# Layer-norm rows turned by DMA transposes of two 16-bit planes instead of TensorE, with the planner's buffers recut

## The chip, the cores and the metric

The kernel runs on one core of one Trainium2 chip. The metric is the device time of one execution in microseconds (us). Three runs of the kernel before took 3198.34, 3198.98 and 3199.27 us; their median, 3198.98 us, is the time before.

## The reference

64 graphs of 256 nodes with 256 features pass through four layers. Every layer begins with the same step, a layer norm over the features and a ReLU; its result goes through a graph network, and that is added to x.

```python
h = jnp.maximum(_layernorm(x, axis=-1), 0.0)
x = x + _L0_gnn_ref(h, adj, ...)     # 4 heads of attention, masked by adj, elu
h = jnp.maximum(_layernorm(x, axis=-1), 0.0)
x = x + _L1_gnn_ref(h, adj, ...)     # 4 heads of attention, a norm of each head
h = jnp.maximum(_layernorm(x, axis=-1), 0.0)
x = x + _L2_gnn_ref(h, adj, ...)     # 1 head of attention over 256 features
h = jnp.maximum(_layernorm(x, axis=-1), 0.0)
x = x + _L3_gnn_ref(h, adj, ...)     # 3 steps: h = GRU(adj^T @ (h @ W_i), h)
```

What matters here is that h is needed turned. It is computed with nodes on the 128 partitions (that is how the norm reduces over features), and the projections and the GRU's gates need the features on the partitions, since TensorE contracts over partitions.

## The kernel before, in words

The 64 graphs are cut into 33 units: the first and the last have one graph, the 31 between have two. `graphs(u, first, nb)` writes down all operations of a unit, with C = 2 nb chunks of 128 nodes. Nothing is issued there: each operation is recorded by `_Schedule.op` with its engine, an estimated cost in ns, the buffers that it reads and writes, and (for a DMA) its bytes. `_Schedule.run` then plays a list schedule over these estimates: on each engine the ready operation with the earliest due date goes next, a buffer of a class (`"xt"`, `"g"`, ...) is taken from a fixed number of slots when its first operation starts and given back when its last one is done, and the instructions are emitted in that order. The order on each of the five engines (TensorE, ScalarE, VectorE, GpSimd, and SyncE, here PE, ACT, DVE, POOL, SP) is therefore fixed in the program, and an instruction that waits holds up everything behind it on its engine. Changed costs or slot counts change the order, not the work.

A unit runs through these steps; several units are in flight, and xt slots bound how many:

- `layer0` loads x into `xt` and the adjacency into `at` by SP, makes the bfloat16 mask `am` and the cap `cap_n`, and turns the latter into `cap` by DMA transposes on SP (L1240, one for each chunk, 128 x 256 of 16 bits, 64 KB).
- `norm(xt, cls)`: DVE statistics (L997, L998), POOL's power (L1006, L1007), one small DVE operation, and ACT's scaled ReLU for each chunk (L1015) into one buffer `xn` (`hn` for the GRU).
- `transposed(xn, cls)`: for each half dc of the features, C turns of 128x128 fp32 on PE into one PSUM bank (L1032), and one ACT copy into `ht`, laid out as [P, DC, S]: half, then node (copies are recorded by the helper `vec`, so they show as L829).
- `project` (L1054): rows of `ht` times weights, two matmuls for each chunk, evicted by ACT into `wh`.
- `factors`: a row of scores is turned (L1111), exponentiated, written to DRAM by ACT's queue (`rd`) and read back by SP as a broadcast over all partitions (`cb`, L1124), for all heads at once. The first two units (`SPREAD`) make it on PE instead (L1092).
- `weights` (L1145, and the minimum with the cap in L829) and `attend_heads` (L1163) form the attention; layers 0, 1 and 2 do norm, turn, project, attend in this way, layers 0 and 1 with 4 heads.
- `gru`: the `hn` of the last norm is turned into the state `ht` and split into two rounded parts `hl` (ACT, then POOL) for `aggregate` (L1361); three GRU steps follow, with gates (L1375, 36 groups of two matmuls of 512 columns in a unit, each of which the trace shows as four passes), turns of the new state (L1389), and the store of `xt` by SP (L1449).

On SP's queue stand the loads of x and the adjacency, the cap transposes, the broadcasts `cb<-rd` and the stores.

## Time and profile before

| what | number |
|---|---|
| median of 3 runs | 3198.98 us |
| span of the profiled execution | 3198.1 us |
| PE MATMUL L1375, gates, 2376 + 2376 passes | 1063.0 + 1055.6 us busy |
| PE MATMUL L1032, turns of xn and hn, 128x128 | 768 + 256 instructions |
| PE idle, 0 to 200 us | 32.3 us |
| PE idle, 3000 to 3198 us | 15.4 us |
| granted PE clock, mean | 0.996 |
| DMA moved | 138.82 MB, mean 43 GB/s |
| cb<-rd loads on SP | 60 of 1024 KB, 30 of 256 KB, 3 smaller |

The page gives one profiled execution. "Busy" is the time in which an engine ran at least one instruction. A group's line has the count, the busy time, the mean of one instruction in ns, and the idle time of the engine ahead of the group with what ended it. For PE the mean is the time from the start of a matmul to its modelled end; matmuls overlap, so the spacing of their starts, which the chain of waits gives, is shorter. A line of the stretch view has the stretch, its length, the busy time and count of PE, PE's weight loads, DVE, ACT and POOL, then the granted PE clock, the DMA engines' share and GB/s.

### The profile page before, as it was taken

The page shows a single profiled execution, that of the slowest core. Times are in us where ns is not written, and L with a number is a line of the kernel's source. Part 1 is how long each engine was busy: PE and PEld are TensorE (multiplying, and loading weights), DVE is VectorE, ACT ScalarE, POOL GpSimd, SP SyncE. Part 2 cuts the span into 40 slices and gives each one's busy share as a digit, 9 for nine tenths or more (in the row PEclk, how much of TensorE's full clock was granted, in tenths as well). Part 3 has the DMA queues.
Part 4 walks back from the last instruction along what each step waited for, and adds up shares of the span by engine and source line. Part 5 has one row for each costly group of instructions (what it writes and reads, how often), then busy time and mean ns, then how long its engine had stood idle before and what let it go on. Part 6 is the DMA issues. An engine that isn't in the chain of part 4 may idle for free.

```text
span 3198.1 us, 48707 instructions
## 1 busy us (share of the span) xinstructions
PE 3143.2 (98%) x18599; PEld 1931.9 (60%) x18599; DVE 2321.4 (73%) x5206; ACT 1486.8 (46%) x3128; POOL 897.4 (28%) x907
## 2 busy tenths in 40 slices
PE   7899999999999999999999999999999999999998
PEld 6765656565666655566656566556566556665555
DVE  7777867778767778767678677788677787677753
ACT  5454444454454444454444454544444444544433
POOL 4323332133331233331233321333311333311210
PEclk9999999999999999999999999999999999999999
DMA  4110111101111101111101111111111011101000
GB/s 129 34 49 29 54 54 34 47 31 50 54 54 34 47 31 50 54 47 34 53 28 54 53 36 45 40 41 54 54 34 47 31 50 50 47 23 44 11 16 12
DMA packets 109927, 138.82 MB, mean 43 GB/s; under 512 B 44714, under 2 KB 97524, under 8 KB 102004
## 3 DMA queue, kind: packets, MB, share of 16 engines
q1 hardware_dynamic: 105712, 134.25, 12.8%
q8 instruction: 149, 2.44, 0.3%
q10 hardware_dynamic: 3972, 1.36, 0.2%
q14 instruction: 94, 0.77, 0.1%
HBM read 109.84 MB, written 17.34 MB: 40 GB/s over the span
## 4 chain that ended last, share of the span: by engine, by line
PE 87%; DVE 9%; POOL 2%; ACT 1%; issue 1%; DMA 0%; SPq 0%; ACTq 0%; POOLq 0%; DVEq 0%
PE bank L1375 55%; PE bank L1054 10%; PE bank L1163 10%; PE bank L1361 5%; PE bank L1032 3%; PE bank L1389 2%; DVE pt L1145 2%; DVE g L829 2%; DVE pt L829 1%; POOL mean L1297 1%; POOL o L829 1%; DVE o L829 1%; ACT ht L829 1%; DVE xt L1308 1%; DVE mean L829 1%
## 5 line engine op out<-in xcount | busy, mean ns | idle before, releaser
L1375 PE MATMUL bank<-ag,wc 128*128 128x512 f32 (+1 forms) x2376 | 1063.0, 582 | 0.0
L1375 PE MATMUL bank<-ht,whh 128*128 128x512 f32 (+1 forms) x2376 | 1055.6, 580 | 2.2 <-ACT g L829 1.3
L829 ACT ACTIVATE g<-bank,bg 128x512 f32<-128x512 f32 (+1 forms) x594 | 395.2, 670 | 713.6 <-PE bank L1375 706.6
L1375 PEld LDWEIGHTS bank<-ag,wc 128*128 128x128 f32 x2376 | 441.4, 190 | 459.2 <-issue 441.1
L1375 PEld LDWEIGHTS bank<-ht,whh 128*128 128x128 f32 x2376 | 435.0, 190 | 438.9 <-issue 424.2
L1006 POOL TENSOR_SCALAR mv<-mv 128x4 f32<-128x4 f32 (+1 forms) x132 | 81.9, 621 | 1428.6 <-DVE mv L998 1383.6
L1145 DVE TENSOR_SCALAR pt<-cb,f 128x256 f32<-128x256 f32 x1152 | 416.9, 430 | 6.0 <-ACT cb L1099 5.2
L1163 PEld LDWEIGHTS bank<-wh,pt 128*64 128x64 f32 (+1 forms) x8704 | 345.6, 142 | 94.4 <-issue 76.1
L829 DVE SCALAR_TENSOR_TENSOR g<-g,g 128x512 f32<-128x512 f32 (+1 forms) x396 | 263.3, 670 | 180.4 <-ACT g L829 180.4
L1163 PE MATMUL bank<-wh,pt 128*64 128x65 f32 (+1 forms) x8704 | 382.0, 233 | 9.7 <-DVE pt L829 5.8
L829 DVE TENSOR_TENSOR pt<-pt,cap 128x1024 f32<-128x1024 f32 (+1 forms) x297 | 341.3, 1193 | 0.1
L829 DVE SCALAR_TENSOR_TENSOR g<-bank,g 128x512 f32<-128x512 f32 (+1 forms) x198 | 129.8, 666 | 280.2 <-PE bank L1375 280.0
L829 DVE SCALAR_TENSOR_TENSOR g<-g,ht 128x512 f32<-128x512 f32 (+1 forms) x198 | 136.5, 689 | 172.0 <-ACT g L829 171.6
L1361 PE MATMUL bank<-am_r,hl 128*128 128x256 f32 x1536 | 238.1, 304 | 0.1
L1015 ACT ACTIVATE xn<-xt,mv 128x256 f32<-128x256 f32 x384 | 197.3, 588 | 72.1 <-DVE mv L829 71.9
L1361 PEld LDWEIGHTS bank<-am_r,hl 128*128 128x128 f32 x1536 | 198.2, 189 | 42.5 <-issue 30.6
L829 ACT COPY ag<-bank 128x512 f32<-128x512 f32 (+1 forms) x198 | 113.4, 573 | 233.4 <-PE bank L1361 230.1
L829 ACT ACTIVATE g<-g,bg 128x512 f32<-128x512 f32 (+1 forms) x198 | 137.6, 709 | 161.6 <-DVE g L829 159.4
L997 DVE BATCH_NORM_STATS2 st<-xt 128x6 f32<-128x256 f32 x512 | 208.1, 406 | 6.4 <-DMA xt<-in_x_dram 6.2
L829 ACT COPY ht<-bank 128x512 f32<-128x512 f32 (+1 forms) x264 | 137.8, 573 | 124.0 <-PE bank L1032 123.8
L1136 POOL MEMSET wh<- 128x16 f32 (+3 forms) x99 | 11.8, 120 | 635.5 <-ACT f L1130 635.5
L1007 POOL TENSOR_TENSOR mv<-mv,nhalf 128x4 f32<-128x4 f32 (+1 forms) x132 | 176.0, 1333 | 11.0
(91 smaller groups left out, 3452.2 us busy)
## 6 DMA issues: line engine op xcount, KB each, us to landing
cb<-rd SPq DMA_DIRECT2D x60, 1024.0 KB
xt<-in_x_dram SPq DMA_DIRECT2D x31, 512.0 KB
at<-in_adj_dram SPq DMA_DIRECT2D x31, 512.0 KB
out_dram<-xt SPq DMA_DIRECT2D x31, 512.0 KB
cb<-rd SPq DMA_DIRECT2D x30, 256.0 KB
cap<-cap_n SPq DMA_TRANSPOSE x128
cb<-rd SPq DMA_DIRECT2D x2, 512.0 KB
rd<-row ACTq DMA_DIRECT2D x60, 8.0 KB
```

What stands on the lines that cost most here:

```text
L829: emit = lambda: fn(*[a() if callable(a) else a for a in args], **kw)
L997: nc.vector.bn_stats(st.tile[:, c, :], xt.tile[:, c, :])
L1006: nc.gpsimd.tensor_scalar(mv.tile[:, 2, :], mv.tile[:, 1, :], 1e-5, None, op0=OP.add)
L1007: nc.gpsimd.tensor_tensor(mv.tile[:, 2, :], mv.tile[:, 2, :], nhalf[:, :C], op=OP.pow)
L1015: op("act", 610, lambda: nc.scalar.activation(xn.tile[:, c, :], xt.tile[:, c, :], AF.Relu, bias=mv.tile[:, 3, c : c + 1], scale=mv.tile[:, ...
L1032: nc.tensor.transpose(ps.tile[:, c * P : (c + 1) * P], xn.tile[:, c, dc * P : (dc + 1) * P], ident)
L1054: nc.tensor.matmul(ps.tile[:, : heads * W], lhsT=ht.tile[:, dc, c * P : (c + 1) * P], rhs=we[:, dc].rearrange("p h w -> p (h w)"), start=( ...
L1145: nc.vector.tensor_scalar(pt.tile[:, b, jc, :].rearrange("p (i n) -> p i n", n=P), cb.tile[:, h, 2 * b : 2 * b + 2, :], f.tile[:, 1, h, c ...
L1163: nc.tensor.matmul(ps[q * Q : (q + 1) * Q], lhsT=pt.tile[:, b, jc, i0 : i0 + Q], rhs=wh.tile[:, h, 2 * b + jc, :w], start=(jc == 0), stop= ...
L1361: nc.tensor.matmul(ps.tile[:, b * N : (b + 1) * N], lhsT=hl.tile[:, k, 2 * b + sc, :], rhs=am.tile[:, 2 * b + sc, :], start=(k == 0 and sc ...
L1375: nc.tensor.matmul(ps.tile[:, :S], lhsT=w[:, dc, g * P : (g + 1) * P], rhs=v.tile[:, dc, :], start=(first and dc == 0), stop=(last and dc ...
L1389: nc.tensor.transpose(ps.tile[:, c * P : (c + 1) * P], ht.tile[:, j, c * P : (c + 1) * P], ident)
```

## The change

From unit 4 on (`TURNED`), the four norms' rows are turned by SP instead of PE. A fp32 word is two 16-bit words. For each graph (two chunks, 128 x 512 words) ACT copies the low halves and the high halves into two planes `pl` (a 16-bit copy at a stride of two), one DMA transpose on SP turns all eight 128x128 blocks of the two planes into `tp` (256 KB), and a second ACT copy joins the planes into `ht`. The bits stay as they were. Units 0 to 3 still turn on PE, with the four turns of a graph in one bank instead of the C turns of a feature half.

Buffers are cut by graph: `norm` gives a list of [P, 2, D] buffers, `ht` is [P, C, DC, P] (chunk, half, node), `project` waits for its own graph's half, the GRU's first `hl` are cut by graph, and the broadcast `cb` is loaded in pieces of two heads. `hn` and the unused `ident_h` go; the slots of xt, am, cap, xn go up; those of cb (in bytes), hl and g go down. Some POOL cost estimates are changed.

```diff
+TURNED = 4
...
-            "xt": (slots, 5), "at": (slots, 1), "am": (slots, 4), "cap": (slots, 3),
-            "cap_n": (slots, 1), "xn": (slots, 2), "ht": (slots, 2), "wh": (slots, 3),
-            "cb4_": (slots, 2), "cb1_": (slots, 1), "pt": (slots, 4), "o": (slots, 2),
-            "ag": (slots, 2), "ht3_": (slots, 3), "hn": (slots, 1),
-            "hl": (slots, 3), "am_r": (slots, 1), "g": (slots, 9), "f": (slots, 6),
+            "xt": (slots, 6), "at": (slots, 1), "am": (slots, 6), "cap": (slots, 4),
+            "cap_n": (slots, 1), "xn": (slots, 4), "ht": (slots, 2), "wh": (slots, 3),
+            "cb2_": (slots, 2), "cb1_": (slots, 1), "pt": (slots, 4), "o": (slots, 2),
+            "ag": (slots, 2), "ht3_": (slots, 3), 
+            "hl": (slots, 2), "am_r": (slots, 1), "g": (slots, 8), "f": (slots, 6),
...
-            "mean": (slots, 4), "rd": (dram, 4), "bank": (banks, 8),
+            "mean": (slots, 4), "pl": (slots, 2), "tp": (slots, 2), "rd": (dram, 4), "bank": (banks, 8),
...
-            xn = buf(cls, [P, C, D])
+            xns = [buf(cls, [P, 2, D]) for _ in range(nb)]
...
-            op("pool", 1350, power, parts(mv, range(C)), [(mv, "r")])
+            op("pool", 700 + 320 * C, power, parts(mv, range(C)), [(mv, "r")])
...
-            ht = buf(cls, [P, DC, S])
+            ht = buf(cls, [P, C, DC, P])
...
+            def turned(b):
+                pl, tp = buf("pl", [P, 2, 2 * D], U16), buf("tp", [P, 2, 2 * D], U16)
+
+                def planes(flat):
+                    return flat.bitcast(U16).rearrange("p (n k) -> p k n", k=2)
+
+                op("act", 1150, lambda: nc.scalar.copy(
+                    pl.tile, planes(xns[b].tile.rearrange("p c d -> p (c d)"))), [xns[b]], [pl])
+                dma("sp", 1 << 18, lambda: nc.sync.dma_start(
+                    tp.tile.rearrange("p k (m n) -> p (k m) n", n=P), pl.tile.rearrange("p k n -> p (k n)"),
+                    transpose=True,
+                ), [pl], [tp], cost=4700)
+                op("act", 1150, lambda: nc.scalar.copy(
+                    planes(ht.tile[:, 2 * b : 2 * b + 2].rearrange("p c d n -> p (c d n)")), tp.tile,
+                ), [tp], [(ht, b)])
+
+            for b in range(nb):
+                (flipped if u < TURNED else turned)(b)
             return ht
...
-                op("pe", 895, emit, [ht, B_we], [ps], takes=[wh])
+                op("pe", 895, emit, [(ht, c // 2), B_we], [ps], takes=[wh])
...
-            cb = buf(f"cb{heads}_", [P, heads, C, P])
+            K = min(heads, 2)
+            cbs = [buf(f"cb{K}_", [P, K, C, P]) for _ in range(heads // K)]
...
-                op("pool", 1350 + 200 * C, power, [], [var])
+                op("pool", 630 + 520 * C, power, [], [var])
...
-                hl = buf("hl", [P, 2, C, P], F32R)
+                hl = buf("hl", [P, 2, C, P] if engine == "dve" else [P, 2, 2, D], F32R)
...
                         nc.tensor.matmul(
-                            ps.tile[:, :S], lhsT=w[:, dc, g * P : (g + 1) * P], rhs=v.tile[:, dc, :],
+                            by_chunk(ps.tile[:, :S]), lhsT=w[:, dc, g * P : (g + 1) * P], rhs=block(v, dc),
...
-            ht = transposed(hn, "ht3_")
+            hls = [split(lambda hn=hn: hn.tile, "pool", [hn]) for hn in hns]
+            ht = transposed(hns, "ht3_")
             ag = buf("ag", [P, DC, S])
             for dc in range(DC):
-                aggregate(ag, split(lambda dc=dc: hn.tile[:, :, dc * P : (dc + 1) * P], "pool", [hn]), dc)
+                aggregate(ag, hls, dc, lambda k, b, sc, dc=dc: hls[b].tile[:, k, sc, dc * P : (dc + 1) * P])
```

## The prediction

> **What bounds the kernel now.** I read the page's busy shares and its chain of waits first, then the costliest groups by shape, then a stretch of the chain in order of time, last the stretches around one set of DMA transposes.
>
> ```profile
> PE 3143.2 (98%) x18599; PEld 1931.9 (60%) x18599; DVE 2321.4 (73%) x5206; ACT 1486.8 (46%) x3128; POOL 897.4 (28%) x907
> ...
> PE 87%; DVE 9%; POOL 2%; ACT 1%; issue 1%; DMA 0%; SPq 0%; ACTq 0%; POOLq 0%; DVEq 0%
> PE bank L1375 55%; PE bank L1054 10%; PE bank L1163 10%; PE bank L1361 5%; PE bank L1032 3%; PE bank L1389 2%; DVE pt L1145 2%; DVE g L829 2%; DVE pt L829 1%; POOL mean L1297 1%; POOL o L829 1%; DVE o L829 1%; ACT ht L829 1%; DVE xt L1308 1
> ```
>
> TensorE is busy 98% and carries 87% of the chain; the turns that the change touches (L1032) are 3% of it. In every 200 us stretch from 200 to 2800 us PE is busy for 199.4 us or more. So a microsecond taken from PE shortens the run, and one put on another engine costs only if PE then waits for it. The pattern repeats every 96.9 us, one unit of two graphs (sets of cap transposes start at 1400.73, 1497.63 and 1594.53).
>
> ```profile
> L1032 PE MATMUL bank<-ident,xn 128*128 128x128 f32 x768 | 104.6, 277 | 16.5 <-ACT xn L1015 16.5
> ...
> L1032 PE MATMUL bank<-ident,hn 128*128 128x128 f32 x256 | 33.9, 273 | 0.3 <-ACT hn L1015 0.2
> L829 ACT COPY ht<-bank 128x512 f32<-128x512 f32 x248 | 132.5, 585 | 119.6 <-PE bank L1032 119.5
> ...
> L1214 ACT ACTIVATE cap_n<-at 128x1024 bf16<-128x1024 int32 x31 | 32.8, 1058 | 16.7 <-DMA cap<-cap_n 16.7
> ```
> ```profile
> 1525.00 0.88 PE bank L1032 x8
> ...
> 1569.47 0.87 PE bank L1032 x8
> ```
>
> The mean of 273 ns is the latency of one turn; they overlap. What counts is spacing: eight take 0.87 us on the chain, 0.109 each.
>
> ```profile
> L1240 SPq DMA_TRANSPOSE cap<-cap_n x128: 1167/1232/2462, 16.0 to 2855.6; - x128
> ```
> ```profile
> 1404.00:1405.00 1.00, 1.00 (x7) 0.86 (x6) 0.97 (x6) 0.00 (x0) 0.00 (x0) 1.00 0.31 66
> 1405.00:1406.00 1.00, 1.00 (x9) 0.94 (x8) 0.97 (x5) 0.00 (x0) 0.00 (x0) 1.00 0.21 40
> 1406.00:1407.00 1.00, 1.00 (x7) 0.73 (x6) 1.00 (x5) 0.45 (x1) 0.00 (x0) 1.00 0.19 42
> 1407.00:1408.00 1.00, 1.00 (x3) 0.38 (x2) 1.00 (x4) 0.14 (x1) 0.00 (x0) 1.00 0.00 0
> ```
> ```profile
> SPq L1124 <- DMA rd<-row: 1977.2, 93, 47.5
> ...
> SPq L1449 <- DVE xt L829: 300.8, 32, 58.0
> ```
>
> A transpose of 64 KB (two blocks of 128x128) holds SP's queue for 1.232 us. The four from 1400.73 are issued by 1405.77; at 1407 the DMA engines (last two columns: share, GB/s) are still, so a landing trails its issue by at most 1.23 us. SP mostly waits, in order, for others.
>
> **Removed from PE.** Units 4 to 31 have two graphs and 4 norms x 8 turns; unit 32 has half: 28 x 32 + 16 = 912 turns x 0.109 = 99.4 us. Bounds: by busy time (138.5 / 1024 = 0.135) 123 us; by the low edge of the chain's 3% (2.5% x 3198.1 x 912/1024) 71. I take spacing, since other matmuls close up to it.
>
> **ACT.** 224 copies of 0.585 and 8 small ones of some 0.38 go: -134 us. Added: 228 blocks (28 x 8 + 4), each with a split and a join of 1024 elements per partition. The nearest row is the 1.058 us of the 128x1024 group: 456 x 1.058 = +482. ACT comes to 1835 us, 59% of 3100. No row shows 16-bit words at a stride; were they twice as slow ACT would come to 2317, 75%, still not the bound. What hides it is PE's own work; uncovered, it costs what is in the chain below.
>
> **SP and DMA.** A block is 256 KB, eight 128x128 pieces, four times the row: 4 x 1.232 = 4.93 us of queue, 228 x 4.93 = 1124 us. Per unit: 8 x 4.93 + 5.04 (cap) + some 7 issues of 0.38 = 47 us of a period that should become 96.9 - 3.5 = 93.4. The engines' share rises by about 0.31 x 39.4 / 93.4 = 0.13 from 0.13 to 0.14. Neither fills. In the built order of a steady period SP has two turns, the at load, three turns, the out store, three turns, three cb loads, xt, four cap transposes, two cb loads. Three turns thus stand behind the store, which waits for another unit's last update of xt, and cb loads stand behind up to three turns (15 us). The cb loads in halves add two issues, 0.8 us, on a half-empty queue.
>
> The Trainium skill speaks against the change: "VectorE: DVE Perf Modes", section "The three transpose paths", puts a 128x128 16-bit transpose at 1309 ns by DMA and 390 by TensorE, and its rules keep DMA for where PSUM is not acceptable as the destination. The trace disagrees with the first (1232 ns for two pieces) and, in a dense stream of fp32, with the second (109 ns spacing). By the page a block would be 10.5 us and a unit 84 + 8 = 92 us of SP, so SP would be as full as PE and the time would stay near 3199 or above; by the row it is 3100. The measured row decides.
>
> **The wait that could be late.** From a unit's last attention rows to the first gate on its hn: reciprocal 0.16, xt 0.47, stats 0.6, power 0.64 + 1.37, mv 0.16, four applies 2.4, split 1.06, two blocks in SP's queue 9.86, landing 1.23, join 1.06 = 19 us. In the built order PE has between those two points: 13 gate groups of 1.72 (four passes of 0.43), w0 projection 3.56, two heads 2.02, two aggregates 1.88, turns 1.0 = 31 us. So 12 us to spare; three turns of another unit ahead (15 us) would use it up. At the end of the run the last unit, one graph, needs about 13 us and has 9 x 1.72 = 15.5. I take 0 in the steady part (bounds -0.8 to +1 us a unit, -22 to +28: below, the period is 96.9 while the spacings of its PE rows sum to about 96.1, and a part of that gap is waits for the copies that go; above, one wait of 1 us a unit) and +2 at the end (0 to 6, a whole late block).
>
> **Strides.** The first GRU layer reads ht in four runs of 128 columns. A column takes 0.85 ns in a 128-wide turn (0.109) and 0.84 in a 512-wide gate (0.43), so run length costs nothing in these rows: 0. DVE reads o and wh in pieces at 703 ns against 707 for the gate product: 0.
>
> **Buffers.** xt and am for six, half-size cb and hl, g at eight: no instruction, only order. A unit's way lengthens by some 7 us (first block) to 12 (second) for each of four norms, 47 at most; six slots instead of five give 6 x 93.4 - 5 x 96.9 = +76 us, so this covers itself. Fewer g and hl could stall DVE; the bound of 1 us a unit above holds that too. At the start other work comes first in the order: 0, bounds of 5 us either way, against 32 us of PE idle in the first 200.
>
> **Sum.** 3198.1 - 99.4 + 2 = 3100.7, in the profiled execution's own span; the median of the runs stands 0.9 above it: 3101.6, said as 3101.
>
> **The rivals.**
> *Turns land late: slower.* The change saves 8 x 0.109 = 0.87 us of PE per norm of two graphs, and there are 114 such norms' worth (912 / 8). From 0.87 us of waiting per norm on it is a loss. The place is SP's queue: turns behind the out store or behind each other. At 2 us a norm the time is 3199 + 114 x 1.13 = 3328. For it: SP runs in order, and the store waited 300.8 us for xt, once 58. Against: 12 us of slack, and SP half empty.
> *Another engine takes part of the chain.* DVE, POOL and ACT hold 12% of it, mostly in stretches where PE is busy 99% all the same: two chains of nearly one length. If half of the saving is taken by them, 3199 - 50 = 3150.
> *More than the turns goes.* With 0.135 per turn, or with the waits for the ht copies gone too (22 us): 3199 - 122 = 3077.
> *It does not do what it says.* The order shows no turns on PE after unit 3's, so this is only the case that PE's clock falls; granted is 1.00 in all steady stretches. Not weighed.
>
> **How the numbers follow.** Forecast 3101, 60%, with its own range 3078 to 3130 (the -22 and the +28); more goes 12%; another engine 14%; late 14%. Most of the late case is above 3199, and 2 of its points lie within 0.2% (6.4 us, about what a measurement here can tell from no change); another engine gives 1 there. So faster 0.85, same 0.03, slower 0.12. The range runs from 3070 to 3160: it takes in the bounds, 3077 and 3150, and leaves out most of the late case.
>
> **What would show it.** Turns: L1032 down to some 112 instructions and PE's busy time lower by 99 to 123 us, PE again at 199 us or more in steady stretches of 200, the period of cap transposes at 93.4. ACT near 1835; each new transpose near 4.93 us on SP, landing about 1.2 later. If PE's groups wait for ACT ht or its join, the late case holds; if a block takes over 10.5 us on SP (8 of them and the rest then fill 93), SP is the bound. I am wrong if steady stretches of PE show more than 1 us idle per unit.

## The result and the profile after

The changed kernel takes 3239.48 us (median of four runs, 3238.88 to 3240.06), against 3199.12 us for the kernel before in the same series: a ratio of 1.0126, 95% interval 1.0111 to 1.014. It is slower by 40 us; the forecast was 98 us faster.

The first view is the page's busy shares and chain of waits.

```profile
span 3237.6 us, 47649 instructions
...
PE 3104.5 (96%) x17687; PEld 1851.3 (57%) x17687; DVE 2416.1 (75%) x5205; ACT 1830.6 (57%) x3346; POOL 875.9 (27%) x905
...
PE 67%; DVE 27%; ACT 2%; issue 2%; POOL 1%; DMA 0%; ACTq 0%; SPq 0%; DVEq 0%; POOLq 0%
```

PE has its 912 turns less, but its busy time fell by only 38.7 us and the span around it grew. DVE, which the change hardly touches, is busy 95 us longer and holds 27% of the chain instead of 9%. The next views are steady stretches of PE (length, busy time and count, granted clock, DMA share, GB/s), one of the kernel before and two of the changed kernel.

```profile
1000.00:1200.00 200.00, 199.65 (x1166) 1.00 0.13 44
```
```profile
1000.00:1200.00 200.00, 194.27 (x1085) 0.98 0.27 65
1600.00:1800.00 200.00, 194.27 (x1092) 1.00 0.26 64
```

PE idles 5.7 us in 200 where it idled 0.35, and the granted clock is no longer 1.00 throughout. What PE waits for (engine, line, releaser: total us, times, longest):

```profile
PE bank L1408 <- ACT ht L1055: 46.0, 25, 2.6
PE bank L1408 <- ACT g L829: 25.4, 45, 1.6
PE bank L1422 <- DVE ht L829: 21.0, 8, 4.5
PE bank L1034 <- ACT xn L1015: 19.2, 4, 9.7
```

The last row is of the first units, which still turn on PE, and is not new (16.5 us before). The largest wait is for the new join (L1055), 25 times, about once a unit: that looks like turns that land late. But the queue's rows (minimum, median and maximum ns) and ACT's rows for split and join say otherwise:

```profile
L1051 SPq DMA_TRANSPOSE tp<-pl x228: 1231/1237/3098, 125.5 to 3156.3; - x114
```
```profile
L1055 ACT COPY ht<-tp 128x1024 uint16<-128x1024 uint16 x228 | 304.4, 1336 | 0.0
L1049 ACT COPY pl<-xn 128x1024 uint16<-128x1024 uint16 x228 | 234.2, 1040 | 0.0
```

A block of 256 KB holds SP's queue for 1.24 us, a quarter of what was reckoned, and ACT is never idle ahead of a join (0.0): the turns are there, the join stands late in ACT's order. The timeline shows what is late (start, length, engine, line, operation; "x7" are seven in a row; in brackets the idle time ahead and what ended it). This stretch comes back every unit.

```profile
1636.07 2.50 POOL L829 TENSOR_TENSOR o<-o,gamma_b 128x512 f32<-128x512 f32 x2
1636.13 1.23 DVE L829 SCALAR_TENSOR_TENSOR mv<-mv 128x4 f32<-128x4 f32 x1 [0.58 <-POOL mv L1007]
...
1639.04 5.25 DVE L1172 TENSOR_SCALAR pt<-cb,f 128x256 f32<-128x256 f32 x7
...
1640.32 2.54 POOL L829 TENSOR_TENSOR o<-o,beta_b 128x512 f32<-128x512 f32 x2
...
1642.81 2.61 POOL L829 TENSOR_TENSOR hl<-xn,hl 128x512 fp32r<-128x512 f32 x2
...
1644.21 1.76 DVE L829 SCALAR_TENSOR_TENSOR g<-g,g 128x512 f32<-128x512 f32 x1
...
1645.90 2.98 DVE L1172 TENSOR_SCALAR pt<-cb,f 128x256 f32<-128x256 f32 x9
1646.07 0.69 ACT L829 ACTIVATE g<-bank,bg 128x512 f32<-128x512 f32 x1 [2.38 <-DVE g L829]
...
1650.65 0.72 ACT L829 ACTIVATE g<-g,bg 128x512 f32<-128x512 f32 x1 [2.66 <-DVE g L829]
...
1652.71 1.33 ACT L1055 COPY ht<-tp 128x1024 uint16<-128x1024 uint16 x1
...
1654.09 1.12 PE L1408 MATMUL bank<-ht,whh 128*128 128x512 f32 x2 [1.86 <-ACT ht L1055]
```

While POOL runs its power, beta and hl, seven weights of DVE take 5.25 us; the nine after POOL has stopped take 2.98 us. The mean of the seven hides two kinds, as the row of the weights alone shows (minimum, median and maximum ns, first and last start), in the changed kernel and in the run e16 below, where POOL waits:

```profile
L1172 DVE TENSOR_SCALAR pt<-cb,f x7: 401/403/1405, 1639.0 to 1642.9; 128x256 f32<-128x256 f32 x7
```
```profile
L1182 DVE TENSOR_SCALAR pt<-cb,f x7: 398/402/403, 1684.0 to 1686.0; 128x256 f32<-128x256 f32 x7
```

The first four start before beta and take 0.40 us each, beside the power too. The three beside beta and hl take 1.35 to 1.41 us, each about as long as one operation of POOL (1.26 to 1.32 us). The same holds over the whole trace of the changed kernel: the 175 weights that overlap one of POOL's long operations (bias, gamma, beta, hl) take 1043 ns in the mean, the other 977 take 409. In the kernel before, 30 of the 1152 meet one.

A gate product takes 1.76 instead of 0.68 us. So DVE is about 4 us late, ACT waits 2.38 and 2.66 us for DVE's gates, the join behind them in ACT's order is late, and PE waits 1.86 us. The price is more than the wait. One period earlier, in stretches of 1 us (after the length the busy time and count of PE, PE's weight loads, DVE, ACT, POOL, then the granted clock, DMA share and GB/s):

```profile
1553.00:1554.00 1.00, 0.44 (x2) 0.00 (x0) 1.00 (x3) 1.00 (x3) 0.00 (x0) 1.00 0.00 0
1554.00:1555.00 1.00, 0.00 (x0) 0.00 (x0) 1.00 (x2) 1.00 (x2) 0.00 (x0) 1.00 0.03 8
1555.00:1556.00 1.00, 0.70 (x2) 0.46 (x3) 0.68 (x2) 1.00 (x3) 0.00 (x0) 1.00 0.07 16
1556.00:1557.00 1.00, 1.00 (x4) 0.52 (x3) 0.96 (x4) 1.00 (x3) 0.00 (x0) 0.84 0.54 109
1557.00:1558.00 1.00, 1.00 (x2) 0.37 (x2) 0.93 (x5) 1.00 (x3) 0.00 (x0) 0.50 0.82 153
...
1559.00:1560.00 1.00, 1.00 (x2) 0.34 (x1) 1.00 (x3) 1.00 (x2) 0.92 (x2) 0.50 0.00 0
1560.00:1561.00 1.00, 1.00 (x4) 0.41 (x3) 1.00 (x3) 0.59 (x1) 0.72 (x1) 0.95 0.00 0
```

After 1.86 us without PE (0.56 + 1.00 + 0.30) the clock falls to 0.50 and comes back in the slice from 1560: about 3.4 us at half speed, some 1.7 us of PE's work lost on top of the wait. Not every such wait does this: after the one at 1654.09, just as long, the clock stays at 1.00. In slices of 4 us, 15 units between 400 and 2800 us show a fall.

That reading left three theories. **A**: the work of POOL and DVE on the port that the plan calls `port` meets, and DVE pays. **B**: the plan's 4.7 us for a block puts joins too late in ACT's order. **C**: the fewer slots of g and hl stall the gates.

### The profile page after: what moved, and what is told of

Same layout as the page of the kernel before. It is cut to its first block, busy times and chain, and to the rows that moved or that the text cites. A ratio compares the mean times of both kernels' runs of the same rounds, so it can differ in the third digit from the quotient of the medians.

```text
span 3237.6 us, 47649 instructions
## 1 busy us (share of the span) xinstructions
PE 3104.5 (96%) x17687; PEld 1851.3 (57%) x17687; DVE 2416.1 (75%) x5205; ACT 1830.6 (57%) x3346; POOL 875.9 (27%) x905
## 4 chain that ended last, share of the span: by engine, by line
PE 67%; DVE 27%; ACT 2%; issue 2%; POOL 1%; DMA 0%; ACTq 0%; SPq 0%; DVEq 0%; POOLq 0%
PE bank L1408 44%; PE bank L1190 8%; PE bank L1073 8%; DVE pt L1172 6%; DVE g L829 5%; PE bank L1387 4%; DVE st L997 3%; DVE xt L829 2%; PE bank L1422 2%; DVE o L829 2%; DVE mv L998 1%; DVE pt L829 1%; DVE mean L829 1%; DVE ht L829 1%; DVE mv L829 1%
## 5 line engine op out<-in xcount | busy, mean ns | idle before, releaser
L1408 PE MATMUL bank<-ht,whh 128*128 128x512 f32 (+1 forms) x2376 | 1087.0, 597 | 49.4 <-ACT ht L1055 46.0
L1408 PE MATMUL bank<-ag,wc 128*128 128x512 f32 (+1 forms) x2376 | 1048.5, 583 | 23.3 <-ACT g L829 23.3
L1408 PEld LDWEIGHTS bank<-ht,whh 128*128 128x128 f32 x2376 | 448.5, 195 | 531.2 <-issue 435.8
L1172 DVE TENSOR_SCALAR pt<-cb,f 128x256 f32<-128x256 f32 x1152 | 501.8, 506 | 80.2 <-PE bank L1190 73.6
L829 DVE SCALAR_TENSOR_TENSOR g<-g,g 128x512 f32<-128x512 f32 (+1 forms) x396 | 303.9, 769 | 175.8 <-ACT g L829 175.8
L1015 ACT ACTIVATE xn<-xt,mv 128x256 f32<-128x256 f32 x512 | 274.2, 594 | 96.3 <-DVE mv L829 92.4
L1055 ACT COPY ht<-tp 128x1024 uint16<-128x1024 uint16 x228 | 304.4, 1336 | 0.0
L1049 ACT COPY pl<-xn 128x1024 uint16<-128x1024 uint16 x228 | 234.2, 1040 | 0.0
L1006 POOL TENSOR_SCALAR mv<-mv 128x4 f32<-128x4 f32 (+1 forms) x132 | 51.5, 390 | 672.5 <-DVE mv L998 607.4
L829 POOL TENSOR_TENSOR o<-o,bias_b 128x512 f32<-128x512 f32 (+1 forms) x66 | 85.8, 1301 | 538.6 <-DVE o L829 538.6
L997 DVE BATCH_NORM_STATS2 st<-xt 128x6 f32<-128x256 f32 x512 | 207.0, 404 | 6.0 <-DMA xt<-in_x_dram 5.7
```

What stands on the lines that cost most here:

```text
L829: emit = lambda: fn(*[a() if callable(a) else a for a in args], **kw)
L997: nc.vector.bn_stats(st.tile[:, c, :], xt.tile[:, c, :])
L1006: nc.gpsimd.tensor_scalar(mv.tile[:, 2, :], mv.tile[:, 1, :], 1e-5, None, op0=OP.add)
L1015: op("act", 610, lambda: nc.scalar.activation(xns[c // 2].tile[:, c % 2, :], xt.tile[:, c, :], AF.Relu, bias=mv.tile[:, 3, c : c + 1], sca ...
L1049: op("act", 1150, lambda: nc.scalar.copy(pl.tile, planes(xns[b].tile.rearrange("p c d -> p (c d)"))), [xns[b]], [pl])
L1055: op("act", 1150, lambda: nc.scalar.copy(planes(ht.tile[:, 2 * b : 2 * b + 2].rearrange("p c d n -> p (c d n)")), tp.tile,), [tp], [(ht, b)])
```

## The experiments

All are edits of the changed kernel unless said otherwise. A "port operation" is one that the code marks `port=True`. The plan starts none while another is running on DVE or POOL (`if (not o.port or self.port_free <= clock) and self.roomy(o)` in `_Schedule.run`), but nothing in the program enforces that on the chip: each engine runs its own order as soon as its operands are there.

| run | us | ratio to before, 95% interval | DVE busy, us |
|---|---|---|---|
| changed kernel | 3239.48 | 1.0111 to 1.014 | 2416.1 |
| e1 turns on PE | 3189.66 | 0.996 to 0.9985 | 2274.9 |
| e2 SP cost 1240 | 3253.55 | 1.0144 to 1.0203 | 2362.8 |
| e5 slots back | 3235.34 | 1.0087 to 1.0146 | 2416.1 |
| e6 POOL narrow | 3123.30 | 0.9738 to 0.9794 | 2274.9 |
| e7 POOL narrow and scratch | 3232.84 | 1.0092 to 1.0126 | 2398.9 |
| e3 POOL costs back | 3205.85 | 1.0014 to 1.0033 | 2359.6 |
| e8 power planned as port | 3237.13 | 1.0107 to 1.0141 | 2378.4 |
| e9 port held in order | 3138.93 | 0.9799 to 0.9832 | 2270.1 |
| e10 and power held | 3358.15 | 1.0483 to 1.0518 | 2274.4 |
| e11 before, port held | 3195.82 | 0.9983 to 1.0002 | 2240.7 |
| e12 true costs, port held | 3172.32 | 0.9903 to 0.9936 | 2255.8 |
| e13 e8 with port held | 3181.18 | 0.9932 to 0.9965 | 2263.0 |
| e14 and addition held | 3145.35 | 0.9815 to 0.9848 | 2262.7 |
| e15 only addition held | 3227.45 | 1.0072 to 1.0106 | 2400.8 |
| e16 only POOL waits | 3125.69 | 0.9754 to 0.9787 | 2302.8 |
| e17 turns on PE, port held | 3185.66 | 0.9945 to 0.9973 | 2243.9 |
| e18 true costs, POOL waits | 3167.80 | 0.9889 to 0.9925 | 2269.7 |
| e19 turns on PE, POOL waits | 3185.83 | 0.9946 to 0.9976 | 2244.2 |

### Four first looks: the turns, the estimate, the slots, POOL's load

**e1: every row turned on PE, the rest of the change kept.**

```diff
-TURNED = 4
+TURNED = 99
```

> The changed kernel with all turns left on TensorE (the unit from which SP turns is set past the last one): buffers by graph, slots, the 8-bit mask and the planner's other estimates stay as changed. Theory A (DVE and POOL meet on their shared port because the new order lets them overlap, whoever turns): DVE's pt group stays near 0.50 us a piece and the time is 3230 or more. Theory B (the turn's joins come late on ACT, since the planner reckons 4.7 us of SP for a transpose that takes 1.24): with no joins the time is 3199 within 10, DVE near 2320 us busy. Theory C (fewer g and hl slots, smaller cb): well over 3199, 3220 or more, with waits for buffers on DVE or ACT.

3189.66 us, PE busy 200.00 of 200 us in steady stretches, DVE back at 2274.9 us. The recut buffers, estimates and order are worth about 8 us by themselves; the loss comes only with the turns off PE. This is what B expected, and it refutes A in the form "whoever turns": with the turns on PE 33 weights meet POOL's long operations, with the turns off it 175.

**e2: SP's estimate set to what the trace shows.**

```diff
-                ), [pl], [tp], cost=4700)
+                ), [pl], [tp], cost=1240)
```

> The changed kernel, the planner told 1240 ns for a block's transpose in place of 4700; nothing else. Theory B: joins move up in ACT's order, PE's waits for the join (46 us by PE, 68 by its weight loads) fall under 20 us and the time falls to 3150 or less. Theory A: DVE's pt group stays near 0.50, joins wait less but the time stays within 3200 to 3250. Theory C: no change, about 3237.

3253.55 us, slower still. The waits for joins are gone, others come in (DVE waits 115.1 us for streamed `cb`), and DVE is still busy 2362.8 us. B, which expected 3150 us or less, is refuted as the whole cause. A fits only in part: the time lies 4 us above its range, and the weights take 440 ns in the mean, not 500.

**e5: the slots of hl and g as before.**

```diff
-            "hl": (slots, 2), "am_r": (slots, 1), "g": (slots, 8), "f": (slots, 6),
+            "hl": (slots, 3), "am_r": (slots, 1), "g": (slots, 9), "f": (slots, 6),
```

> The changed kernel with hl at 3 and g at 9 slots again, as before the change. Theory C: 3180 or less. Theories A and B: within 30 us of 3239, in either direction, as the order changes by chance.

3235.34 us, the same within the intervals, where C expected 3180 or less. C is refuted.

**e6: POOL's bias, gamma and beta of the first layer cut to 16 elements of a partition.** Order and estimates are unchanged. Most of these three operations is left out.

```diff
-                vec(nc.gpsimd.tensor_tensor, pool(1290), lambda: o.tile[:, hs], lambda: o.tile[:, hs],
-                    lambda: each(gamma_b), op=OP.mult, reads=[B_gamma], writes=part, engine="pool", port=True)
+                vec(nc.gpsimd.tensor_tensor, pool(1290), lambda: o.tile[:, hs, :1, :8], lambda: o.tile[:, hs, :1, :8],
+                    lambda: each(gamma_b)[:, :, :1, :8], op=OP.mult, reads=[B_gamma], writes=part, engine="pool", port=True)
```

> The changed kernel in the very same order on all engines, but POOL's bias, gamma and beta of layer 1 touch 16 elements in place of 512 (the rest of the product with gamma and of the sums is left out; these inputs have gamma one, bias and beta zero). It takes some 245 us of POOL's port use away. Theory A: DVE's pt group goes back to some 0.43 us, DVE's busy time falls by 60 us or more, PE's idle in the steady stretches falls from 5.7 to under 3 us per 200, and the time falls by 50 us or more. Theory B: the joins still stand behind ACT's other work and the time falls by less than 25. Theory C: by less than 25.

3123.30 us, 116 us under the changed kernel; DVE 141 us less busy; the weights take 431 ns in the mean and PE idles under 0.7 of 200 us, as A expected. This fits A, but also another reading: gamma and beta stand on a chain that ends at hl, and the cut made POOL's results earlier.

**e7: the load put back, the earliness kept.** Full-width additions on a scratch tile that nobody reads, one after the bias and two after the beta, follow the cut operations. Left out is the same as in e6.

```diff
+    def scratch(n, w):
+        for _ in range(n):
+            nc.gpsimd.tensor_tensor(scr[:, :w], scr[:, :w], scr[:, :w], op=OP.add)
...
+                op("pool", pool(1290), lambda: narrow((beta_b,), (OP.add,), 2), [B_beta], part, port=True)
```

> The changed kernel in its own order on every engine; as in the run before, POOL's first-layer bias, gamma and beta touch 16 elements of a partition each, but now three full-width adds on a scratch tile that nobody waits for stand in POOL's queue: one after the bias, two after the beta. POOL's load on the port it shares with DVE is thus back (about 2.5 us for each add under contention, 0.7 more us of DVE for each port operation that meets one), while the results that PE's chain needs from POOL come about 5 us earlier than in the changed kernel. Left out: bias, gamma and beta of the first layer on all but 16 elements. Theory A (what costs the time is DVE being slowed by POOL's port work): DVE's busy time back to 2380-2420 us, the transposes of DVE back to about 500 ns, and 3200 to 3245 us. Rival A2 (what costs the time is POOL's own lateness: gamma and beta stood 10 us on the chain before hl, and the narrow run took them out): the time stays within 3115 to 3150 us although DVE's busy time goes back up. In between, both count, shared out in proportion.

3232.84 us and DVE at 2398.9 us: nearly all of the loss comes back through operations that no one waits for. So the lateness of bias, gamma and beta is not the cause; the meeting is, or the lateness of what follows in POOL's queue (hl), which the scratch work brings back as well. e16 below separates these two. The two pages, e6 and then e7:

```profile
PE 3057.5 (98%) x17687; PEld 1842.0 (59%) x17687; DVE 2274.9 (73%) x5205; ACT 1827.2 (59%) x3346; POOL 672.2 (22%) x905
```
```profile
PE 3092.5 (96%) x17687; PEld 1852.5 (57%) x17687; DVE 2398.9 (74%) x5205; ACT 1825.0 (56%) x3346; POOL 892.1 (28%) x1104
```

POOL's scratch work costs DVE 124 us of busy time and PE 35 us, though neither has an instruction more.

### Better estimates, or the plan's order enforced

**e3: the old estimates of POOL's work and of the mask's transposes; e8: the power operations counted as port users.** Both change only the order. Of e3 the first of four such lines is shown, of e8 the first of two.

```diff
-            op("pool", 700 + 320 * C, power, parts(mv, range(C)), [(mv, "r")])
+            op("pool", 1350, power, parts(mv, range(C)), [(mv, "r")])
```
```diff
-            op("pool", 700 + 320 * C, power, parts(mv, range(C)), [(mv, "r")])
+            op("pool", 680 + 150 * C, power, parts(mv, range(C)), [(mv, "r")], port=True)
```

> The changed kernel with the planner's estimates of POOL's power operations, of the mask's negation and of the mask transposes as they stood before the change; only the order changes. Theory A (port contention that the plan doesn't see): the order shifts, the contention stays, 3190 to 3260 us with DVE busy over 2350 us and DVE's first-layer power-chain operation on POOL still over 1000 ns in the mean. Rival D (the new estimates themselves put POOL's work at a bad place): DVE falls to about 2300 us, PE is above 199 us of 200 and the time is 3100 to 3140 us.

> The changed kernel with POOL's power operations counted in the plan as users of the port that POOL shares with DVE, at 680+150 and 700+420 ns a row group instead of 700+320 and 630+520 (about what they take alone); the planner then puts no DVE port operation beside them. Nothing else changes but the order. Theory A: if most of the contention starts at the power operations (3.6 us in place of 0.31 us, after which everything on POOL is 3.3 us late), it goes down: DVE busy 2300 to 2340 us, the mean-row operation on POOL under 700 ns, and 3110 to 3180 us. If the drift between plan and chip has other sources, contention stays as it is and the time is 3200 to 3260 us. Rival B (joins misplaced in ACT's order): unchanged contention or not, joins still wait and the time is above 3200 us.

3205.85 and 3237.13 us. Both orders still collide (DVE 2359.6 and 2378.4 us). The order of the old estimates costs 34 us less than that of the new ones, but it doesn't end the collisions. In both runs the addition ahead of POOL's first-layer power takes 203 ns in the median, against a mean of 1578 in the changed kernel, so e3's expectation of over 1000 ns is not met, nor is e8's that the collisions go when this addition is short.

**e9: the port kept in the plan's order by semaphores.** Each DVE port operation waits for the last POOL port operation that the plan has before it, and the other way round.

```diff
+        other = {"dve": "pool", "pool": "dve"}.get(o.engine)
+        if o.port and other in self.held and k < len(traced):
+            self.tc.add_manual_dep(
+                traced[k], self.held[other],
+                mybir.DependencyInfo(mybir.DependencyClass.Sync, mybir.DependencyReason.DATA),
+                reason="port",
+            )
+        if o.port and k < len(traced):
+            self.held[o.engine] = traced[-1].name
```

> The changed kernel in its own planned order, but with a semaphore wait between each DVE port operation and the last POOL port operation that stands before it in the plan, and the other way round, so that the two engines use the port in the plan's order. (The power operations aren't counted, as in the plan.) Theory A: gamma, beta and bias fall from about 2500 to about 1300 ns, DVE's busy time to 2300-2330 us, and DVE waits for POOL instead, by 1 to 2 us a block; if being slowed is dearer than waiting, 3120 to 3190 us; if waiting costs DVE as much as being slowed, 3220 to 3260 us and the cause is then that POOL is late, not that the two share the port. Rival B: as the changed kernel, 3230 to 3245 us.

3138.93 us: the whole computation, the same order on every engine, 100 us less by waits alone, and no weight meets a long operation of POOL any more. The expectation reads 2.50 us as the time of one gamma, but the timeline's row has two: the changed kernel's mean is 1313 ns, e9's 1237. What falls is DVE's busy time, further than expected.

**e10: POOL's power operations take part too.**

```diff
+            op("pool", 700 + 320 * C, power, parts(mv, range(C)), [(mv, "r")], hold=True)
```

> As the run with the port kept in the plan's order by semaphores, and POOL's power operations (norms and first layer) take part in it too; planned order and estimates are unchanged. Theory A: what is left of the contention there (the mean-row operation of POOL 1565 ns in the mean, 310 ns alone) goes, that operation falls under 600 ns, PE's 1.1 us of idle per 200 us shrinks, and the time is 3118 to 3137 us. Rival (waiting is now as dear as being slowed): the operation falls as said, but DVE's waits for POOL rise by as much, and the time is 3137 to 3165 us.

3358.15 us, a miss. The collisions are gone (addition 203 ns, gamma and beta near 1240), but DVE now stands behind the power itself. POOL's rows, and what DVE's weights wait for:

```profile
L1017 POOL TENSOR_TENSOR mv<-mv,nhalf 128x4 f32<-128x4 f32 (+1 forms) x132 | 133.9, 1015 | 11.0
L1333 POOL TENSOR_TENSOR mean<-mean,nhalf 128x8 f32<-128x8 f32 (+1 forms) x66 | 105.7, 1601 | 5.5
L1332 POOL TENSOR_SCALAR mean<-mean 128x8 f32<-128x8 f32 (+1 forms) x66 | 13.4, 203 | 160.1 <-DVE g L839 60.0 <-DVE ht L839 55.2 <-DVE mean L839 26.0
```
```profile
DVE g L839 <- POOL mv L1017: 67.0, 57, 1.5
DVE ht L839 <- POOL mean L1333: 53.0, 26, 2.0
DVE pt L1182 <- POOL mv L1017: 43.8, 30, 1.6
```

A power lasts 1.0 to 1.6 us on 4 or 8 elements of a partition, and waits of DVE that the plan had no room for went through to PE. With the turns off PE, lost time of DVE costs, whether by slowing or by waiting.

**e11, e12, e13: a control, and two other orders with the port held.** The edit is that of e9, on the kernel before, on the changed kernel with 1240, 1040 and 1340 ns for block, split and join, and on e8.

> A control: the kernel before with the same semaphores between DVE's and POOL's port operations, in its own order. Theory A (the contention became dear with the change, since before it PE never waited for DVE): DVE's busy time falls from 2321 to about 2280 us, but PE, busy 199.65 of 200 us, has nothing to gain: 3190 to 3202 us. Rival F (keeping the port in order is a gain of its own that has nothing to do with the change): under 3175 us.

> The changed kernel with the durations that its trace shows in the plan (SP 1.24 us a block, ACT's split 1.04 and join 1.34 us) and the port kept in the plan's order by semaphores. Theory A (the wrong SP estimate is harmless, and the earlier run with 1.24 us was slower by the same contention in another order): 3120 to 3160 us. Rival B (joins stand too late in ACT's order because of the 4.7 us estimate, and this was hidden by the contention): under 3118 us. Rival G (the order that the true estimate makes is bad of itself, DVE waits 115 us for streamed blocks in it): over 3185 us.

> The run that counted POOL's power operations as port users in the plan (3237 us), with the port kept in the plan's order by semaphores. Theory A: that run was slow only because the chip drifted from the plan; kept in order it is 3110 to 3150 us, with DVE's busy time under 2280 us and the mean-row operation under 600 ns. Rival (its order was slow for another reason, PE's waits for DVE and for ACT's gates): over 3190 us.

e11 is not told from the kernel before: DVE gives back 81 us and the time doesn't move, since PE has no idle time to lose. The same waits are worth 100 us only once the turns are off PE. e12 and e13, 3172 and 3181 us, lie above A's ranges and below those of the rivals that call the order itself bad (over 3185 and over 3190); e12's rival B, under 3118 us, is refuted. The waits help there too: e13 is 56 us under e8, the same order without them, and e12 81 us under e2, whose plan differs by the two ACT estimates.

### What starts the collisions, and which wait pays

**e14, e15, e16.** e14 is e9 plus the short addition ahead of each power; e15 holds only that addition (the first diff, of the first layer's power; the norms' has the same). e16 is e9 with POOL waiting for DVE, but DVE never for POOL (the second).

```diff
-                op("pool", 630 + 520 * C, power, [], [var])
+                op("pool", 630 + 520 * C, power, [], [var], hold="first")
```
```diff
-        if o.port and other in self.held and k < len(traced):
+        if o.port and o.engine == "pool" and other in self.held and k < len(traced):
```

> As the run with the bulk port operations kept in the plan's order (3139 us), and of POOL's power operations only the first instruction (adding epsilon, 0.2 to 0.3 us alone), not the power itself of 1.0 to 1.6 us behind it. Theory A with its amendment (the run that held the whole power operation, 3358 us, lost by making DVE wait out 134 + 106 us of powers that need no port): the mean-row addition falls from 1565 to about 200 ns, PE's idle of 1.1 us per 200 us shrinks, 3115 to 3140 us. Rival W (any wait that the plan has no room for is paid in full by PE, however short): DVE waits 198 more times, 3150 to 3250 us.

> The changed kernel in its own order; semaphores keep only the first instruction of POOL's power operations in the plan's order with DVE's port operations; bias, gamma, beta and hl run into DVE's work as they come. Theory A1 (the loss starts where DVE's back-to-back port work holds up POOL's 0.3 us addition for 3.6 us, and the collisions of gamma, beta and hl follow from that lateness): 3120 to 3170 us with DVE's busy time under 2320 us. Theory A2 (the bulk operations collide by themselves, since POOL is early or late for many reasons): 3200 to 3300 us with DVE's busy time over 2370 us.

> As the run with the bulk port operations kept in the plan's order (3139 us), but only POOL waits for DVE's port operations; DVE never waits for POOL. Theory A2 (what matters is that POOL doesn't begin its bulk work in a DVE burst that the plan has before it): most of the gain stays, 3135 to 3170 us, DVE's busy time 2290 to 2340 us. Rival (the half that matters is DVE not beginning a port operation while POOL's gamma, beta or bias is running, where each is slowed by 0.4 us and DVE's chain is the one that PE waits for): 3190 to 3245 us.

e14: the addition falls from 1565 to 202 ns, and the time is 3145.35 us, 6 us over e9 and just outside A's range. e15: the addition is at 202 ns too, and the time 3227.45 us, as A2 has it. So POOL's long addition, which I had taken for the start of the trouble, accounts for about 12 us by this run. e16: 3125.69 us, better than A2 expected and the best version that computes everything. Here is e16 in the same stretch of a unit as shown above for the changed kernel:

```profile
1681.06 2.50 POOL L839 TENSOR_TENSOR o<-o,gamma_b 128x512 f32<-128x512 f32 x2
...
1684.03 2.34 DVE L1182 TENSOR_SCALAR pt<-cb,f 128x256 f32<-128x256 f32 x7
...
1686.29 0.68 DVE L839 SCALAR_TENSOR_TENSOR g<-g,g 128x512 f32<-128x512 f32 x1
...
1686.89 2.98 DVE L1182 TENSOR_SCALAR pt<-cb,f 128x256 f32<-128x256 f32 x9
...
1691.09 1.26 POOL L839 TENSOR_TENSOR o<-o,beta_b 128x512 f32<-128x512 f32 x1 [5.65 <-DVE pt L839]
...
1693.91 1.35 ACT L1065 COPY ht<-tp 128x1024 uint16<-128x1024 uint16 x1
```

Gamma still meets DVE's `mv`, but beta, which followed it after 1.75 us, now waits 5.65 us for weights that stand before it in the plan. The seven weights take 2.34 instead of 5.25 us, the product 0.68 instead of 1.76; from the weights to the join it is 9.88 us instead of 13.67. So POOL had not been late: it ran **ahead** of the plan, into DVE's burst. This also answers what e7 left: beta and hl wait longer here than in the changed kernel, and the time falls. The rows of beta, changed kernel and then e16 (idle time ahead of it at the end):

```profile
L829 POOL TENSOR_TENSOR o<-o,beta_b 128x512 f32<-128x512 f32 (+1 forms) x66 | 87.2, 1337 | 0.4
```
```profile
L839 POOL TENSOR_TENSOR o<-o,beta_b 128x512 f32<-128x512 f32 (+1 forms) x66 | 82.9, 1260 | 189.2 <-DVE pt L839 142.0 <-DVE xt L1344 28.9 <-DVE g L839 12.5
```

189 us of waiting ahead of beta on POOL, which has the time, and smaller waits ahead of its other long operations make the run 113.8 us shorter. Only 3 weights still meet one. PE's steady stretches in e16:

```profile
1000.00:1200.00 200.00, 199.42 (x1178) 1.00 0.27 65
1600.00:1800.00 200.00, 199.42 (x1125) 1.00 0.27 67
```

### The turns' own worth

**e17, e19: e1 with the port held both ways (the edit of e9), and with POOL alone waiting (that of e16); e18: e12 with POOL alone waiting.**

> All turns back on PE (the first experiment, 3190 us) with the port kept in the plan's order: the same contention-free state as the 3139 us run, so that the difference of the two is what turning by DMA is worth by itself. If a turn on PE is worth the 109 ns that the forecast reckoned, the difference is near 99 us and this run would be near 3238 us, which the 200.00 of 200 us that PE was busy without the semaphores excludes; by PE's busy sums (3131.6 against 3064.7 us, 0.073 us a turn) it is 3185 to 3195 us and the worth 46 to 60 us.

> The changed kernel with the durations of its trace in the plan (SP 1.24 us a block, split 1.04, join 1.34 us), and only POOL waiting for DVE's port operations, never DVE for POOL. Theory A2 (POOL's waits give nearly all of the gain; the estimate of SP by itself isn't what cost the time): 3140 to 3172 us, a little under the run with both waits (3172 us), and still behind the 3126 us of the plan with the 4.7 us estimate, since in this order DVE waits some 106 us for streamed blocks. Rival B (the true estimates make the better plan once the port is out of the way): under 3126 us.

> All turns on PE, and only POOL waiting for DVE's port operations: the counterpart of the 3126 us run. Theory: PE is the bound here and has nothing to gain, 3182 to 3190 us as with both waits (3186 us); the difference to 3126 us, 56 to 64 us, is then the worth of the 912 turns by themselves, 61 to 70 ns each, against the 109 ns of the forecast. Rival (the semaphores' one-sided form is a gain of its own, whatever turns the rows): under 3165 us.

e17: 3185.66 us. e18: 3167.80 us, so the true costs of block, split and join make the worse order here also when POOL waits (DVE waits 107.1 us for `cb`). e19: 3185.83 us; against e16 the 912 turns are worth 60.1 us, 66 ns each. By PE's busy sums (3129.2 against 3060.6 us) they free 68.6 us, 75 ns each.

## Why the prediction was wrong

**What bounds the kernel: right, but not for long.** PE was the bound, and e11 shows it: taking 81 us off DVE moved nothing. The prediction took from this that a microsecond on another engine costs only if PE waits for it, and then never reckoned what DVE's and POOL's own work would cost each other once PE was shorter. It named the case (another engine takes part of the chain) and priced it at half the saving, 3150 us.

**The step that failed: "I take 0 in the steady part", bounds -0.8 to +1 us a unit.** PE idled 5.7 us in 200, about 2.8 us a unit, against the more than 1 us that it named as its own refutation. The cover of 12 us that this step counted was for a chain through SP; the chain that came late runs through DVE's bursts, ACT's gates and the join behind them. In the step's place the runs showed POOL's bulk operations starting in the middle of DVE's bursts: e7 puts the cost back with work that nobody waits for, e16 takes 113.8 us away by making POOL wait. Of the 136.9 us by which the span missed (3237.6 against 3100.7), that is 113.5. Between the spans of the changed kernel and e16 (3237.6 and 3124.1 us), 69.6 us are PE's idle time (133.1 against 63.5) and 43.9 us its longer busy time for the same instructions, of which the granted clock, 0.982 in the mean against 0.993, explains some 36 us (0.018 x 3237.6 less 0.007 x 3124.1, an estimate).

**PE, -99.4 us: too large, the second step that failed.** The spacing of eight turns in the chain gave 109 ns each. Freed were 75 ns each by busy time and 66 in the run's time, 68.6 and 60.1 us, below the lower bound of 71. The kernel without turns on PE also idles there 8.7 us more (63.5 in e16 against 54.8 in e19). The price of a turn was not the error. Added up from the starts of the matmuls (from one start to the next, less idle time), the turns take 116.0 us in e19 and 16.3 in e16: 99.7 us go, 109 ns for each. But in e16 the other matmuls stand 31 us further apart in sum, gates 31 and aggregates -19 among them. "Other matmuls close up to it" is what failed. Why they don't was not tried; the two runs also differ in order.

**ACT, 1835 us: right**, 1830.6 measured, though not term by term: the split took 1040 ns and the join 1336, not 1058 each, so 538.6 us were added and not 482. What makes up for it is overlap: in the trace an ACT operation starts before the one ahead of it has ended, and busy time counts this once. These overlaps sum to 162.2 us before and 228.0 after, which the prediction did not reckon.

**SP, 4.93 us a block: a quarter of that**, 1.237 us. Scaling a queue's time with bytes was wrong. No harm is seen from it: the DMA engines' share is 0.26 as forecast, and SP holds 0% of the chain. The estimate from the 1309 ns of the Trainium skill ("VectorE: DVE Perf Modes", "The three transpose paths"), 10.5 us a block, is not what this trace shows either. The row is the time for which the queue is held; when a block lands it does not say, and ACT's joins show only that the blocks were there in time.

**Buffers: nearly as forecast.** e5 gives 3235 us with the slots back, 4 us less within overlapping intervals; e1 shows the recut as a gain of some 8 us, where 0 was taken. The prediction did not speak of the mask `am`, which the change also stores in 8 bits; the mean of the cast to `am_r` grew from 681 to 767 ns, but by the collisions and not by the 8 bits: with the port held it is 690 ns in e9.

**The rivals.** *Turns land late* had the right sign and a wrong place: ACT was never idle ahead of a join and SP holds 0% of the chain; the joins were late, behind ACT's waits for DVE. PE did wait for the join (46.0 us), which the prediction had named as the sign of this case, so that sign can't tell a late block from a late join. *Another engine takes part* was the right mechanism, at over twice its price. *More goes* was refuted.

**How the forecast misses 3101 when most collisions are gone.** e16's span is 23.4 us above the forecast one (3124.1 against 3100.7): 16.8 us because PE's busy time is 3060.6 and not 3043.8 us, and 6.6 us of idle time of PE (63.5 us against 54.9 before, less the 2 allowed for). Some collisions are left in e16: its DVE is 32.7 us busier than e9's.

**What stays open.** Collisions are older than the change: the waits take 81 us of busy time off DVE in the kernel before (2321.4 to 2240.7), 31 off e1 (2274.9 to 2243.9) and 146 off the changed kernel (2416.1 to 2270.1). Why the chip drifts from this plan so that POOL gets ahead of DVE, and why more with the turns off PE than on it, stays open; e3 shows that the estimates behind the order have a part in it (34 us).

## What to carry to other kernels

A plan that keeps two engines off a shared resource only on paper holds as long as neither runs ahead; when a change makes the bounding engine shorter, look for the pairs that will now meet, and make the engine with time to spare wait, not the one on the chain (POOL alone waiting 3126 us, both 3139, none 3239). Read a wait of PE back to what its releaser waited for: the join looked like a late DMA, and DVE was at fault. Price an operation by its bytes only where two sizes in the trace show that it grows with them.

## What the runs showed of the hardware that was not expected

- A DMA transpose of 256 KB holds SP's queue for 1.237 us, one of 64 KB in the same kernel for 1.19 us (median of the 12 between 1400 and 1700 us).
- Where DVE and POOL meet in the changed kernel, POOL's bulk operations nearly keep their time (means of 1301 to 1351 ns, against 1236 to 1291 in e9) and DVE's stretch (409 to 1043 ns for a weight in the mean, 0.68 to 1.76 us for a product). Not all of DVE's do: its statistics (L997) take 405 ns beside them and 404 elsewhere. In the other direction, two gammas of e1 took 4.07 us at 1640.82, and an addition of POOL's that had taken 0.31 us (at 1623.35) took 3.60 us at 1626.29, while DVE ran six products of 0.64 us back to back (1626.11 to 1629.81 us).
- The Trainium skill ("SBUF — State Buffer", "Who interferes with whom") calls the pair of ports that these two engines share an exclusive lock, which whoever issues first keeps for the whole instruction. DVE's weights, each stretched to about the length of one POOL operation, beside POOL's nearly unstretched ones agree; the addition that lasted over six DVE products, not one, is more than the sentence says.
- PE's clock fell to 0.50 for about 3.4 us after 1.86 us without a matmul (and gaps of 0.26 and 0.71 us in the 12 us ahead of it), in some units and not in others: in the unit shown, gaps of 0.32, 0.71 and 1.86 us left it at 1.00. The Trainium skill ("TensorE: Matmul & The Clock Gate", "HAM oscillation — how this bites in real kernels") asks for no idle gap above about 3.4 us, and tells of a kernel whose frequent micro-idles between groups of matmuls made the clock go down and up; here gaps of at most 1.86 us were enough.
- An ACT copy of 1024 16-bit elements took 1040 ns reading at a stride of two and 1336 ns writing at it.
